# A two-layer Perceiver on one core: layer 0's start and order of work, and the last context chunk's values

## The chip, the cores and the metric

The kernel runs on one core of a Trainium2 chip. A core has five engines that work side by side and meet only through semaphores: TensorE (PE in the profile, its weight loads PEld), VectorE (DVE), ScalarE (ACT), GpSimd (POOL) and SyncE (SP), which here only issues DMAs. The metric is the device time of one execution in microseconds; before the change it is 2798.18 us, the median of 3 runs (2798.04 to 2798.63). All data are float32.

## The reference

The input is `x` (256 rows of 512) and a context of 25088 rows of 512. Two layers follow, each of three residual steps on a layer-normalized `x`. Cut to what matters:

```python
# layer 0
x = x + norm(x) @ W1.T + context.mean(0) @ W2.T + b              # "cross attention": a mean
x = x + banded_self_attention(norm(x))                            # 16 heads, window 128
x = x + moe(norm(x))                                              # 16 experts, top 4 of 2 groups of 4, and a shared one
# layer 1
q, K, V = norm(x) @ Wq + bq, context @ Wk + bk, context @ Wv + bv # 25088 keys, 16 heads of 32
x = x + softmax_over_queries(q K^T / sqrt(32)) V @ Wo + bo        # the softmax runs over the 256 queries
x = x + shifted_window_attention(norm(x))
x = x + moe2(norm(x))                                             # 8 experts, top 2
```

Because the softmax of layer 1's cross attention runs over the queries, each block of keys can be finished by itself: its probabilities are exact as soon as its scores are there, and all blocks are added.

## The kernel before, in words

**Context chunks.** The context is cut into 49 chunks of 512 rows. A chunk's keys and its values are each a 512 x 512 by 512 x 512 product, done as a 2 x 2 block product with seven half-size products instead of eight (`seven`, L528). One such product (`times`, L532) is 4 matmuls of 256 columns; an fp32 matmul leaves two records in the profile. The sums and differences of the context's blocks (`ts`) are made on GpSimd (`chunk_sums`, L517), those of the weight's blocks once on VectorE (`load_weights`, L492), in a tile `wq7` with seven blocks side by side; VectorE adds each product into its one or two targets (L559), GpSimd adds one bias difference (L563).

**Stage A, until about 186 us.** Layer 0 needs the mean over the whole context. Every chunk is loaded once for its column sums (`load_sum`, `chunk_sum`, ScalarE, L579) into buffers `ct` (three, used to the end of the context work) or `cs` (two); between them the keys and values of chunks 0 to 6 (`FIRST = 7`) are made from buffers `ck` (two) and stored to DRAM. Loads are issued by SyncE, stores by GpSimd.

**Stage B, layer 0.** The mean and `norm(x)` are multiplied with `l0x_w` (8 and 8 matmuls of 512 columns, L684). The self attention (`self_attention`, L218) and the expert layer follow. Chunks 7 and 8 (`NPRE = 9` in all) are made meanwhile, by a generator `early_rest`; `early_fill(n)` takes 2n products from it, at places where TensorE would have to wait for VectorE or ScalarE. The router picks the experts in order of their load: `slots` (L792) counts rows by expert with `low` and `ones`, ranks the counts and writes `expert_i`, by which SyncE addresses the loads of the experts' weights. `slots` is called inside the shared expert's `hidden` (L731), after its first third.

**Stage C, layer 1's cross attention.** 49 x 4 blocks of 128 keys, each in two halves of eight heads: 392 half-blocks. Each has 8 score matmuls (L1021), 8 exponentials on ScalarE (L1035) and 8 matmuls with the values (L1048). Between them run the products of chunks 9 to 48 (`projections`): a planner counts them in groups of 1, 2, 1, 2, 1 products and draws the lowest slopes under which each chunk's keys and values are made by the half-block that needs them (`due`, `plan`); values are due two half-blocks into their chunk. Chunk 48 is last, so its values are due at half-block 386.

**What sets the order.** Instructions written with `queue <<` keep their program order on their engine. All others (most VectorE work outside Stage C, all loads) are placed on their engine by a scheduler when their inputs and buffers are ready in its own simulation, lower in the program meaning lower priority; on the chip each engine then runs its list in that order. So a load may be issued before loads that are written ahead of it. Memory pools are opened and closed in scopes; a pool that takes memory of a closed one waits for that one's users. TensorE's list is written out nearly whole with `queue <<`.

Of the kernel before, what the change touches and what calls it, by code (L numbers as in the profile page):

```python
# [15 lines left out]
P = 128  # L16
# [21 lines left out]
def perceiver_kernel(  # L38
# [59 lines left out]
    def load_rows(pool, first, last):  # L98
# [15 lines left out]
    ident = const.tile([P, P], F32, name="ident")  # L114
    make_identity(nc, ident)
    eps = const.tile([P, 1], F32, name="eps")
    nc.vector.memset(eps, LN_EPS)

    tri = const.tile([P, NE0, NE0], F32, name="tri")
    nc.gpsimd.memset(tri, 1.0)  # L120
    nc.gpsimd.affine_select(
        out=tri, in_=tri, compare_op=ALU.is_ge, fill=0.0, base=-1,
        pattern=[[1, NE0], [-1, NE0]], channel_multiplier=0,
    )

    low, ones = (const.tile([P, P], F32, name=n) for n in ("low", "ones"))
    nc.gpsimd.memset(ones, 1.0)
    nc.gpsimd.affine_select(
        out=low, in_=ones, compare_op=ALU.is_ge, fill=0.0, base=-1,
        pattern=[[1, P]], channel_multiplier=-1,  # L130
    )
    iota = const.tile([P, P], F32, name="iota")

    band = const.tile([P, 2 * P], F32, name="band")
    nc.gpsimd.memset(band, 0.0)
    nc.gpsimd.affine_select(
        out=band, in_=band, compare_op=ALU.is_ge, fill=-1e30, base=-1,
        pattern=[[1, 2 * P]], channel_multiplier=-1,
    )
    nc.gpsimd.affine_select(  # L140
        out=band, in_=band, compare_op=ALU.is_ge, fill=-1e30, base=P,
        pattern=[[-1, 2 * P]], channel_multiplier=1,
    )
# [331 lines left out]
    ps = ps_mm([P, P])  # L475
    queue << nc.tensor.matmul(ps, ones, low, start=True, stop=True)
    nc.vector.tensor_copy(iota, ps)

# [10 lines left out]
    wq7 = kvp.tile([P, 2, 7, 2, HB], F32, name="wq7", bufs=1)  # L489
    W_A11, W_A12, W_A22, W_S1, W_S2, W_S3, W_S4 = range(7)  # L490

    def load_weights(k, matrix, ct=None, c=None):  # L492

        a21 = early.tile([P, 2, HB], F32, tag="a21", name="a21")
        for to, i, j in ((wq7[:, k, W_A11], 0, 0), (a21, 1, 0), (wq7[:, k, W_A22], 1, 1), (wq7[:, k, W_A12], 0, 1)):
            nc.sync.dma_start(out=to, in_=l1x_w_d[:, matrix, 2 * j : 2 * j + 2, HB * i : HB * (i + 1)])
            if ct is not None:
                nc.sync.dma_start(out=quarter(ct, j, i), in_=quarter(ctx_d[c], j, i))
        w = wq7[:, k]
        nc.vector.tensor_add(w[:, W_S1], a21, w[:, W_A22])  # L500
        nc.vector.tensor_sub(w[:, W_S2], w[:, W_S1], w[:, W_A11])
        nc.vector.tensor_sub(w[:, W_S3], w[:, W_A11], a21)
        nc.vector.tensor_sub(w[:, W_S4], w[:, W_A12], w[:, W_S2])
# [24 lines left out]
    def seven(ct, ts, out, is_key):  # L528

        w = wq7[:, 0 if is_key else 1]  # L530

        def times(a, b):  # L532
            ps, home = take("kv", [P, 2, HB])
            fixed, moving = (w[:, a], b) if is_key else (b, w[:, a])
# [55 lines left out]
    def early_load(c):  # L590
        if c < FIRST:
            ct = early.tile([P, DC, JC], F32, tag="ck", name="ck")
        else:
            ct = ctp.tile([P, DC, JC], F32, tag="ct", name="ct")
# [41 lines left out]
    early_load(1)  # L636
    rest = list(range(FIRST, NCH))
    for c in range(FIRST):
        units = early_chunk(c)
        n = min(8, len(rest)) if c + 1 < FIRST else len(rest)  # L640
# [7 lines left out]
        if c + 2 < FIRST:  # L648
            early_load(c + 2)
    early_scope.close()  # L650

    def early_rest():
        early_load(FIRST)
        for c in range(FIRST, NPRE):
            if c + 1 < NPRE:
                early_load(c + 1)
            yield from early_chunk(c)
# [7 lines left out]
    l0a_scope = ExitStack()  # L665
    l0w = l0a_scope.enter_context(tc.tile_pool(name="l0w", bufs=1))
    l0a_wo = l0w.tile([P, DC, D], F32, name="l0a_wo")
    with tc.tile_pool(name="l0xw", bufs=1) as l0xw:
        l0x_w = l0xw.tile([P, 2 * DC, D], F32, name="l0x_w")
        nc.sync.dma_start(out=l0x_w, in_=l0x_w_d)  # L670
        nc.sync.dma_start(out=l0a_wo, in_=l0a_wo_d)

        cmean = const.tile([P, DC], F32, name="cmean")
        nc.vector.tensor_reduce(cmean, csum, AX.X, ALU.add)
        nc.vector.tensor_scalar(cmean, cmean, 1.0 / (NCH * JC), None, ALU.mult)
        cmean_b = l0xw.tile([P, DC, P], F32, name="cmean_b")
        nc.vector.tensor_copy(cmean_b, cmean.unsqueeze(2).to_broadcast([P, DC, P]))

        xT = norm_T()
        pss = [ps_mm() for _ in range(T)]  # L680
        for k in range(2 * DC):
            for t in range(T):
                lhsT = xT[:, k, t * P : (t + 1) * P] if k < DC else cmean_b[:, k - DC, :]
                queue << nc.tensor.matmul(pss[t], lhsT, l0x_w[:, k, :], start=k == 0, stop=k == 2 * DC - 1)  # L684
        for t in range(T):
            add_rows(t, pss[t], R_L0X_B)
# [18 lines left out]

    NDENSE = (4 * NT) // (P + 1)
# [23 lines left out]
    def hidden(weights, between=lambda: None):  # L730
        w1, w3, w2 = weights  # L731
        hT = moe0.tile([P, IC0, NT], F32, tag="hT0", name="hT0")
        for ic in range(IC0):
# [10 lines left out]
            if ic == 0:  # L744
                between()
# [40 lines left out]
    early_fill(NPRE * 7)  # L786
# [662 lines left out]
```

## Time and profile before

| | |
|---|---|
| median of 3 runs | 2798.18 us (2798.04 to 2798.63) |
| the profiled execution: its time, its span | 2799.3 us, 2797.6 us |
| mean granted TensorE clock over the span | 0.987 |
| TensorE busy | 2721.9 us (97%) |
| VectorE, ScalarE, GpSimd busy | 1721.7, 1700.9, 577.5 us |
| DMA, mean | 94 GB/s; 422 GB/s from 20 to 160 us |
| Stage A, Stage B, Stage C | to 186 us, to 570 us, to 2455 us |

A line of waits tells which engine waited, at which line and for which tile, after the arrow who ended the wait, and the total, the number and the longest of the waits. A line of the timeline gives the start, the length, the engine, the line, the operation, output<-input and how many; in brackets the engine's idle time before it and what ended it. A line of stretches gives from:to, the length, the busy time and records of each engine, the granted TensorE clock, the DMA share and GB/s. Busy time of TensorE is modelled for pipelined matmuls, so the spacing of starts is the better measure of what a matmul costs.

### The profile page before, as it was taken

What the parts mean: (1) busy time and instruction counts of PE and PEld (TensorE: products, weight loads), DVE (VectorE), ACT (ScalarE), POOL (GpSimd) and SP (SyncE); (2) the same over time, 40 slices, a digit from 0 to 9 for tenths busy, and PEclk for the clock granted to TensorE, in tenths of its full rate; (3) what the DMA queues carried; (4) which work ended last, traced back from release to release, by engine and by line L of the source; (5) the groups of instructions that cost most, each with busy time, mean ns of one, the idle gap of its engine ahead of it and who ended that gap; (6) DMA issues with size and microseconds to landing.
All of it is one profiled execution on the core that took longest, in us unless ns stands there. A gap on an engine that the chain in (4) does not pass through costs nothing. (4 is left out here: it accounts for less than half of the span.)

```text
span 2797.6 us, 57238 instructions
## 1 busy us (share of the span) xinstructions
PE 2721.9 (97%) x21502; PEld 1920.9 (69%) x21502; DVE 1721.7 (62%) x3052; ACT 1700.9 (61%) x7001; POOL 577.5 (21%) x529
## 2 busy tenths in 40 slices
PE   8998899999999999999999999999999999979997
PEld 7866777776666666666666666666666666656775
DVE  4436512267777777777777777777777777742101
ACT  6832100037877777777777778777887778831111
POOL 4321000023222223222222232222222323100000
PEclk9999999999999999999999999999999999989999
DMA  9961344421100101000101000101000100107673
GB/s 387 423 266 76 134 160 170 162 91 41 37 32 32 41 22 47 32 32 32 46 17 47 32 32 32 46 17 47 32 32 32 47 17 27 51 24 297 259 271 145
DMA packets 40869, 262.87 MB, mean 94 GB/s; under 512 B 5320, under 2 KB 8440, under 8 KB 13200
## 3 DMA queue, kind: packets, MB, share of 16 engines
q1 hardware_dynamic: 37408, 237.85, 22.6%
q0 software_dynamic: 3184, 21.33, 1.9%
q8 instruction: 175, 2.87, 0.4%
q14 instruction: 102, 0.84, 0.1%
HBM read 239.23 MB, written 19.40 MB: 92 GB/s over the span
## 5 line engine op out<-in xcount | busy, mean ns | idle before, releaser
L1035 ACT ACTIVATE e<-ps_sc,nm 128x256 f32<-128x256 f32 x3136 | 1437.8, 485 | 377.4 <-DVE nm L1030 376.9
L1030 DVE TENSOR_REDUCE nm<-ps_sc 128x2 f32<-128x512 f32 x1568 | 995.3, 686 | 358.0 <-PE ps_sc L1021 357.9
L1035 ACT ACTIVATION_READ_ACCUMULATOR e<-ps_sc,nm 128x1 f32 x3136 | 678.7, 216 | 0.0
L1048 PE MATMUL ps_ac<-e,vs 128*32 128x256 f32 x6272 | 420.7, 386 | 4.1 <-POOL vs L1062 4.1
L537 PE MATMUL ps_kv<-ts,wq 128*128 128x256 f32 x1568 | 387.1, 391 | 5.8 <-POOL ts L523 5.8
L537 PE MATMUL ps_kv<-wq,ts 128*128 128x256 f32 x1568 | 388.8, 392 | 0.0
L1062 POOL TENSOR_TENSOR vs<-v,rc 128x512 f32<-128x512 f32 x160 | 167.8, 1049 | 1016.3 <-DVE rc L1056 1016.3
L537 PEld LDWEIGHTS ps_kv<-ts,wq 128*128 128x128 f32 x1568 | 286.1, 190 | 91.1 <-issue 27.3
L537 PEld LDWEIGHTS ps_kv<-wq,ts 128*128 128x128 f32 x1568 | 287.2, 191 | 85.2 <-issue 26.5
L1021 PE MATMUL ps_sc<-qT,kT 32*128 32x256 f32 x4096 | 304.1, 401 | 1.5 <-ACT e L1035 1.3
L1048 PEld LDWEIGHTS ps_ac<-e,vs 128*32 128x32 f32 x6272 | 164.2, 109 | 202.2 <-issue 114.1
L559 DVE TENSOR_TENSOR v<-v,ps_kv 128x512 f32<-128x512 f32 x343 | 227.7, 677 | 82.6 <-PE ps_kv L537 58.1
L1021 PEld LDWEIGHTS ps_sc<-qT,kT 32*128 32x128 f32 x4096 | 191.4, 184 | 116.5 <-ACT e L1035 106.4
L537 PE MATMUL ps_kv<-wq,ct 128*128 128x256 f32 x1008 | 244.2, 385 | 0.0
L537 PE MATMUL ps_kv<-ct,wq 128*128 128x256 f32 x1008 | 242.4, 383 | 0.0
L559 DVE TENSOR_TENSOR kT<-kT,ps_kv 128x512 f32<-128x512 f32 x280 | 187.1, 681 | 68.4 <-PE ps_kv L537 58.4
L537 PEld LDWEIGHTS ps_kv<-wq,ct 128*128 128x128 f32 x1008 | 189.7, 191 | 38.2 <-ACT e L1035 12.9
L537 PEld LDWEIGHTS ps_kv<-ct,wq 128*128 128x128 f32 x1008 | 188.1, 190 | 38.1 <-ACT e L1035 12.6
L1338 ACT ACTIVATE hT<-ps_mm,b 128x128 f32<-128x128 f32 x128 | 36.6, 368 | 210.5 <-PE ps_mm L1332 157.3
L1021 PE MATMUL ps_sc<-qT,kTp 32*128 32x256 f32 x2176 | 156.9, 400 | 0.0
L523 POOL TENSOR_TENSOR ts<-ct 128x512 f32<-128x512 f32 x84 | 107.1, 1275 | 230.9 <-DMA ct<-in_ctx_dram 230.9
L1021 PEld LDWEIGHTS ps_sc<-qT,kTp 32*128 32x128 f32 x2176 | 99.6, 184 | 58.7 <-ACT e L1035 55.2
(273 smaller groups left out, 2180.2 us busy)
## 6 DMA issues: line engine op xcount, KB each, us to landing
ct<-in_ctx_dram SPq DMA_DIRECT2D x67, 1024.0 KB, 5.0
we<-in_l1e_dram SPq DMA_DIRECT2D x64, 1024.0 KB, 6.8
we<-in_l0e_dram SPq DMA_DIRECT2D x17, 1536.0 KB, 8.1
cs<-in_ctx_dram SPq DMA_DIRECT2D x17, 1024.0 KB, 14.6
we0o<-in_l0e_dram SPq DMA_DIRECT2D x17, 768.0 KB, 4.5
kv<-kT POOLq DMA_DIRECT2D x9, 1024.0 KB, 9.7
kv<-v POOLq DMA_DIRECT2D x9, 1024.0 KB, 9.4
vp<-kv SPq DMA_DIRECT2D x9, 1024.0 KB, 4.8
```

Source lines behind the costliest of these rows:

```text
L523: queue << nc.gpsimd.tensor_sub(ts[:, k], a, b)
L537: queue << nc.tensor.matmul(ps[:, m, :], fixed[:, d, m * P : (m + 1) * P], moving[:, d, :], start=d == 0, stop=d == 1,)
L559: queue << nc.vector.tensor_tensor(to, old, ps, ALU.subtract if a == W_A22 else ALU.add)
L1021: queue << nc.tensor.matmul(sc[r][:, i, :], kTs[c][part, 2 * qp + i, s * P : (s + 1) * P], qT[part, 2 * qp + i, :], start=True, stop=True,)
L1030: queue << nc.vector.tensor_reduce(nm[:, 2 * qp : 2 * qp + 2, r], sc[r], AX.X, ALU.max, negate=True)
L1035: queue << nc.scalar.activation(e[:, 4 * i + r, :], sc[r][:, i, :], AF.Exp, bias=nm[:, q, r : r + 1], accum_out=sm[:, q, r : r + 1],)
L1048: queue << nc.tensor.matmul(acc[qp][32 * r : 32 * r + 32, i, :], v[:, h * HD : (h + 1) * HD], es[qp][:, 4 * i + r, :], start=first and i = ...
L1062: queue << nc.gpsimd.tensor_mul(vs.rearrange("p (h d) -> p h d", h=H), vs_of[c, s].rearrange("p (h d) -> p h d", h=H), rc.unsqueeze(2).to_ ...
L1338: nc.scalar.activation(hT[:, fc, :], ps[:, fc, :], AF.Gelu, bias=b1[:, hf * FC + fc : hf * FC + fc + 1])
```

## The change

It does the following.

- `load_weights` loads each weight, and chunk 0 with it, in two halves of 256 input rows in place of four quarters. The quarters are now read in place, out of a tile `whole`; only the four sums are kept apart (`sums`). The seven blocks side by side and the tiles `a21` go.
- The constants for GpSimd (`ident`, `tri`, `low`, `ones`, `band`) are made by `make_constants`, called after the first loads have been written. The small product that makes `iota` moves from the kernel's start to behind the self attention.
- Chunk 6 leaves the loop of Stage A: its buffer is a `ct`, and its 14 products are now the first of `early_rest`.
- The pools of `l0a_wo` and `l0x_w` are opened before that loop. After it `norm_T` transposes `norm(x)`, nine products of chunk 6 run, then the product of `norm(x)` with `l0x_w`, row block by row block. The mean is multiplied once (4 matmuls) and added to both row blocks, in place of a product for each. Its broadcast lies in a `tmp` buffer.
- In the expert layer four products run, then `slots`, then all products left, then the shared expert. `picked` shares `gt`'s buffer. The copy of `to` goes from VectorE to ScalarE.
- The values of chunk 48 are made block by block: 8 products of 4 matmuls (128 keys, 256 columns) in place of seven, in groups of one, the two of each block due by the block's end.

```diff
-    ident = const.tile([P, P], F32, name="ident")
-    make_identity(nc, ident)
...
+    def make_constants():
+        make_identity(nc, ident)
+
+        nc.gpsimd.memset(tri, 1.0)
...
-    ps = ps_mm([P, P])
-    queue << nc.tensor.matmul(ps, ones, low, start=True, stop=True)
-    nc.vector.tensor_copy(iota, ps)
...
-    wq7 = kvp.tile([P, 2, 7, 2, HB], F32, name="wq7", bufs=1)
+    whole = [kvp.tile([P, DC, D], F32, name=f"whole{k}", bufs=1) for k in range(2)]
+    sums = [kvp.tile([P, 4, 2, HB], F32, name=f"sums{k}", bufs=1) for k in range(2)]
...
+    def weight(k, a):
+        if a >= W_S1:
+            return sums[k][:, a - W_S1]
+        return quarter(whole[k], int(a == W_A12 or a == W_A22), int(a == W_A22))
...
-        a21 = early.tile([P, 2, HB], F32, tag="a21", name="a21")
-        for to, i, j in ((wq7[:, k, W_A11], 0, 0), (a21, 1, 0), (wq7[:, k, W_A22], 1, 1), (wq7[:, k, W_A12], 0, 1)):
-            nc.sync.dma_start(out=to, in_=l1x_w_d[:, matrix, 2 * j : 2 * j + 2, HB * i : HB * (i + 1)])
+        for j in range(2):
+            half = slice(2 * j, 2 * j + 2)
+            nc.sync.dma_start(out=whole[k][:, half, :], in_=l1x_w_d[:, matrix, half, :])
             if ct is not None:
-                nc.sync.dma_start(out=quarter(ct, j, i), in_=quarter(ctx_d[c], j, i))
...
+                nc.sync.dma_start(out=ct[:, half, :], in_=ctx_d[c][:, half, :])
+        a21 = quarter(whole[k], 0, 1)
...
     def early_load(c):
-        if c < FIRST:
+        if c + 1 < FIRST:
             ct = early.tile([P, DC, JC], F32, tag="ck", name="ck")
...
     early_load(1)
+    make_constants()
+    l0a_scope = ExitStack()
+    l0w = l0a_scope.enter_context(tc.tile_pool(name="l0w", bufs=1))
+    l0a_wo = l0w.tile([P, DC, D], F32, name="l0a_wo")
+    l0xw_scope = ExitStack()
+    l0xw = l0xw_scope.enter_context(tc.tile_pool(name="l0xw", bufs=1))
+    l0x_w = l0xw.tile([P, 2 * DC, D], F32, name="l0x_w")
     rest = list(range(FIRST, NCH))
-    for c in range(FIRST):
+    for c in range(FIRST - 1):
...
+    nc.sync.dma_start(out=l0x_w, in_=l0x_w_d)
+    early_load(FIRST)
+
+    xT = norm_T()
+
     def early_rest():
-        early_load(FIRST)
+        yield from early_chunk(FIRST - 1)
...
-        pss = [ps_mm() for _ in range(T)]
-        for k in range(2 * DC):
-            for t in range(T):
-                lhsT = xT[:, k, t * P : (t + 1) * P] if k < DC else cmean_b[:, k - DC, :]
-                queue << nc.tensor.matmul(pss[t], lhsT, l0x_w[:, k, :], start=k == 0, stop=k == 2 * DC - 1)
-        for t in range(T):
-            add_rows(t, pss[t], R_L0X_B)
+    for _ in range(9):
+        next(unmade)
+
+
+    for t in range(T):
+        ps = ps_mm()
+        for k in range(DC):
+            queue << nc.tensor.matmul(
+                ps, xT[:, k, t * P : (t + 1) * P], l0x_w[:, k, :], start=k == 0, stop=k == DC - 1
+            )
+        add_rows(t, ps, R_L0X_B)
+
+    nc.sync.dma_start(out=l0a_wo, in_=l0a_wo_d)
...
+    cmean_b = work.tile([P, D], F32, tag="tmp", name="cmean_b").rearrange("p (c j) -> p c j", c=DC)
+    nc.vector.tensor_copy(cmean_b, cmean.unsqueeze(2).to_broadcast([P, DC, P]))
+    ps = ps_mm()
+    for k in range(DC):
+        queue << nc.tensor.matmul(ps, cmean_b[:, k, :], l0x_w[:, DC + k, :], start=k == 0, stop=k == DC - 1)
+    for t in range(T):
+        nc.vector.tensor_add(x[:, t, :], x[:, t, :], ps)
+    l0xw_scope.close()
...
+    ps = ps_mm([P, P])
+    queue << nc.tensor.matmul(ps, ones, low, start=True, stop=True)
+    nc.vector.tensor_copy(iota, ps)
...
-    early_fill(NPRE * 7)
-    store()
+    early_fill(2)
...
-        picked = mini([P, T, NE0, NE0], "picked")
+        picked = moe0.tile([P, T, NE0, NE0], F32, tag=f"gt{NE0}", name="picked", bufs=1)
...
-    pending = [*hidden(shared_weights, between=slots), None]
+    slots()
+    early_fill(NPRE * 7)
+    store()
+    pending = [*hidden(shared_weights), None]
...
-        nc.vector.tensor_copy(to, tp)
+        nc.scalar.copy(to, tp)
...
+        def values_by_block(c, ct, v):
+
+            for s in range(SUB):
+                for j in range(2):
+                    half = slice(HB * j, HB * (j + 1))
+                    ps, home = take("kv", [P, HB])
+                    for d in range(DC):
+                        queue << nc.tensor.matmul(
+                            ps, ct[:, d, s * P : (s + 1) * P], whole[1][:, d, half],
+                            start=d == 0, stop=d == DC - 1,
+                        )
+                    queue << nc.vector.tensor_add(v[:, s, half], ps, rows[R_L1X_BV][:, half])
+                    give(home)
+                    if j == 1:
+                        made.add(("v", c, s))
+                    yield
...
+                if k + 1 == len(late):
+                    yield from values_by_block(c, cts[k], v)
+                    break
...
-        groups, done = (1, 2, 1, 2, 1), 0
-        total = 2 * len(groups) * len(late)
+        groups, done = (1, 2, 1, 2, 1) * (2 * len(late) - 1) + (1,) * (2 * SUB), 0
+        total = len(groups)
...
-                due += [(2 * SUB * at, k + len(groups)), (2 * SUB * at + 2, k + 2 * len(groups))]
+                k = 10 * (c - NPRE)
+                due.append((2 * SUB * at, k + 5))
+                if c == late[-1]:
+                    due += [(2 * SUB * at + 2 * s, k + 5 + 2 * s) for s in range(1, SUB + 1)]
+                else:
+                    due.append((2 * SUB * at + 2, k + 10))
```

## Prediction

> **What bounds the kernel now.** I read the page first, for the engine that is full:
>
> ```profile
> span 2797.6 us, 57238 instructions
> PE 2721.9 (97%) x21502; PEld 1920.9 (69%) x21502; DVE 1721.7 (62%) x3052; ACT 1700.9 (61%) x7001; POOL 577.5 (21%) x529
> ...
> PE   8998899999999999999999999999999999979997
> ```
>
> TensorE is busy nearly all the time, so time is won only by removing TensorE work or one of its few gaps; a faster VectorE or GpSimd buys nothing by itself. The low digits lie in slices 1, 4 to 6 and 37, that is at the start, around 180 to 350 us and after the context attention. Next, TensorE's waits, whose columns are line, tile, releaser, then total, times and longest:
>
> ```profile
> PE ps_mm L737 <- DMA we<-in_l0e_dram: 6.3, 1, 6.3
> PE ps_mm L476 <- POOL low L128: 6.1, 1, 6.1
> PE ps_kv L537 <- POOL ts L523: 5.8, 2, 5.4
> PE ps_mm L684 <- issue: 5.3, 1, 5.3
> PE ps_ac L1048 <- POOL vs L1062: 4.1, 1, 4.1
> PE ps_mm L198 <- DMA l0a_wqkv<-in_l0a_wqkv_dram: 3.4, 1, 3.4
> ```
>
> All six touch edited code. The 5.3 at L684 is put down to issue, but the load of `l0x_w` was issued at 185.06 and lands 7.5 us later, at 192.6; the matmul starts at 192.81. It is that load. The third view is busy time by stretch (PE, PEld, DVE, ACT, POOL, clock, DMA share, GB/s):
>
> ```profile
> 150.00:160.00 10.00, 10.00 (x48) 8.81 (x47) 2.50 (x4) 8.33 (x28) 0.00 (x0) 1.00 1.01 423
> 186.00:193.00 7.00, 1.72 (x13) 1.38 (x12) 1.91 (x4) 0.00 (x0) 0.00 (x0) 0.89 0.82 300
> 193.00:199.50 6.50, 6.50 (x10) 2.68 (x11) 0.00 (x0) 0.00 (x0) 0.00 (x0) 0.59 0.00 0
> 199.50:209.30 9.80, 9.80 (x24) 4.34 (x23) 0.62 (x1) 0.00 (x0) 0.00 (x0) 1.00 0.01 2
> 338.00:350.00 12.00, 5.72 (x18) 4.71 (x18) 1.73 (x8) 0.38 (x1) 0.00 (x0) 0.72 0.98 390
> ```
>
> In the context stage DMA is as full as TensorE (1.01). After a gap the granted clock is 0.59: 10 matmuls in 6.5 us, then 24 in 9.8. A gap is paid twice.
>
> **Units.** An fp32 matmul leaves two records. One product of `seven` (8 records, 256 columns) takes 1.73 us (0.216 each); a 512-column record takes 0.43.
>
> **Part 1, start and context stream: 3.7 us.** The first product starts at 6.71, the second at 15.72, waiting for `ts` and then at half clock; from 21.56 on products follow each other every 1.73. Afterwards nothing waits for `low`, and the first four loads are halves. The quarters flowed at 302, 210, 165, 242, 277, 301, 323, 361 GB/s in the eight us from 2 to 10, where whole chunks give 422; DMA share 0.99 gave 323. With 6 issues (0.5 us each) in place of 12 and longer rows I take 400, so 1 MB more has come by 10 us: the stream is 2.4 us ahead. Both halves of both operands land near 9. GpSimd now issues the 0.56 us row load before its constants, which end near 8.0 in place of 7.36; two subtractions of 1.28 put `ts1` at 10.6, the second product near 11, and the fourth near 15 to 16, some 5.5 us sooner.
> The SBUF page of the Trainium skill (SBUF — State Buffer, section The DMA setup-cost knee) speaks against larger pieces where the first bytes count: fixed 2 us plus bytes at 436 GB/s. By it the first pair of quarters is there at 0.82 + 2 + 1.2 = 4.0, a pair of halves at 5.2, a loss of 1.2 us. The row puts the first product at 6.71, and the second, which needs nearly all pieces, at 15.72, so I go by the row.
> TensorE can't keep the 5.5, since the stream bounds chunk 6:
>
> ```profile
> 143.34 0.68 SPq L598 DMA_DIRECT2D ck<-in_ctx_dram  x1
> ...
> 160.15 1.27 POOL L523 TENSOR_TENSOR ts<-ck 128x512 f32<-128x512 f32 x1 [16.71 <-PE ps_kv L537]
> ...
> 163.94 1.99 PE L537 MATMUL ps_kv<-ts,wq 128*128 128x256 f32 x8 [0.42 <-POOL ts L523]
> ```
>
> It lands at 160 for use at 161.4. In a `ct` buffer it takes the place issued at 146.06 but has the same loads ahead; with the stream 2.4 ahead, it lands near 157.5. Two subtractions later (160.2) its second product starts, not at 163.94: 3.7. Below: -2 if chunk 6 lands 5 us late; above: 6.
>
> **Part 2, the mean's turn: 12.5 us.** The 8 transposes (1.04 us) now run before chunk 6, where TensorE would wait anyway: 1.0. Then nine products bring TensorE to 174. `l0x_w` no longer waits for the early buffers (SyncE waited 19.4 us there); behind the last sum it lands at 168 to 174, as `l0a_wo`, issued at 151.35, landed at 167.5. Gone: the gap, 5.3, and the slow clock, 16.5 us for 32 records at 0.43 = 13.7, so 2.8. The TensorE page of the Trainium skill (TensorE: Matmul & The Clock Gate, section HAM oscillation) charges about 1.7 us of half rate per such wait, which would give 0.9 lost in place of 2.8; the row decides. Mean product: 4 matmuls in place of 8, 8 x 0.43 = 3.4. The column sums, their broadcast and two added VectorE sums (0.69 each, one replaced bias addition less) lie beside the x products. If `l0x_w` is late, everything behind it in TensorE's fixed order is, by the same time: range 4 to 8.1 for that term.
>
> **Part 3, qkv weights: 1.4 us.** Issued at 209.53 after L684's last read, used at 220.68; `xT` was ready at 218.5, so 2.2 are to be had. The narrower `l0xw` pool may let it go ahead of the mean product; I can't see the placement: 0 to 2.2, two chances in three, 1.4. The attention keeps 18 products in the same places, one phase of `seven` earlier: no change, plus or minus 3 (its 3.1 us wait for VectorE at 274 may move).
>
> **Part 4, routing: 8.2 us.** The experts' load leaves at 336.95, 1 us after `expert_i`, and lands at 344.3; TensorE waits 6.3 from 338 and then takes 12.64 us for 48 records worth 10.35: 2.3 more. Now four products cover the choice (`sel` at 322.1, products until 323.1), the counting follows, and seven products (12.1) plus the whole shared hidden layer (10.4) come after it. VectorE's chain took 5.0 us, so `expert_i` is there by 330 and the weights by 338.5; TensorE wants them at 347. 8.6, less 0.4 for a possible wait for `sel`. Ends: 2 (VectorE puts the products' additions first) and 8.6. `picked` in `gt`'s buffer stays on one engine: nothing. The copy of `to` on ScalarE: 0.42 on VectorE, 0.37 for L289's like form: nothing. `iota`'s product moves, 0.25 us, no sum.
>
> **Part 5, the last chunk: 7.0 us.**
>
> ```profile
> 2405.59 1.07 PE L1048 MATMUL ps_ac<-e,vs 128*32 128x256 f32 x16
> ...
> 2411.32 1.07 PE L1048 MATMUL ps_ac<-e,vs 128*32 128x256 f32 x16
> ...
> 2415.32 1.07 PE L1048 MATMUL ps_ac<-e,vs 128*32 128x256 f32 x16
> ...
> 2434.73 1.07 PE L1048 MATMUL ps_ac<-e,vs 128*32 128x256 f32 x16
> ...
> 2438.38 1.07 PE L1048 MATMUL ps_ac<-e,vs 128*32 128x256 f32 x16
> ...
> 2451.68 3.31 PE L1048 MATMUL ps_ac<-e,vs 128*32 128x256 f32 x32 [4.05 <-POOL vs L1062]
> ```
>
> A half-block with two products takes 5.73, with one 4.00, without any 3.65 (2434.73 to 2438.38), which is ScalarE's eight exponentials, though TensorE's own work is 2.08. Values due by half-block 386 leave six without products. The plan is the same up to half-block 346; then 40 half-blocks held 40 groups, 16 of them double (40 x 4.00 + 16 x 1.73 = 187.7, as the trace has it), and six ran at ScalarE's pace (24 us from 2426.09 to the last exponential, 2449.96). Afterwards 46 hold 43 groups, 14 double, three empty: 43 x 4.00 + 14 x 1.73 + 3 x 2.08 + 1.5 for ScalarE's debt = 204, and 1.6 to the last exponential. 187.7 + 23.9 - 205.6 = 6.0, the eighth product (1.73) included. TensorE's last wait shrinks below 3 us, so the final 32 records need 2.3 in place of 3.3: 1.0. The third `wct` load now waits for the last chunk's buffer until near 2442; 5.5 us later it is there, used past 2480: hidden.
>
> **Sum.** 3.7 + 12.5 + 1.4 + 8.2 + 7.0 = 32.8. The profiled run took 2799.3 (span 2797.6), 1.1 over the median of the runs shown. 2798.2 - 32.8 = 2765.4; I say 2766.
>
> **Rivals.** (a) *The stream takes it back.* `l0x_w` and `l0a_wo` (3.1 MB) need no early buffer now and may be issued ahead of chunk 6: 3.1 MB at 422 GB/s is 7.4 us, and a long gap brings 2.8 of slow clock: 2766 + 10 = 2776. For it: share 1.01. Against: `l0a_wo` was issued behind the last sum. 20%. (b) *The routing wait stays*, because additions delay the slot chain on VectorE, or waits in layer 0's attention grow: 2766 + 8 = 2774; 10%. (c) *Slower.* The weight quarters are now read with a row stride of 512 in place of packed. Three of seven products use them, 49 chunks x 2 x 3 = 294. If each cost over 0.11 us more (6%), the 32.8 is gone; at 0.15 it ends at 2766 + 44 = 2810. Against: `ct` quarters are strided so today, and L537's forms with `ct` and with `ts` take 385 and 391 ns. With anything else of that sign 7%. (d) *No change:* 2%. (e) *More*, chunk 6 earlier and attention smoother: 2756, 3%. The main case has 58%, own range 2757 to 2775.
>
> **From this** the range is 2754 to 2784, with (a) and (b) inside and nearly all of (c) outside. A measurement of this kernel tells about 0.2%: faster 0.90, same 0.03, slower 0.07.
>
> **What would show it.** Right: no 6 us wait at L737's later place, none over 1 us for `l0x_w`; second product near 11; chunk 6's second product near 160; half-blocks of 4.0 to the end of L1048. Wrong: DMA waits of L537 on `ts` or `ct` between 130 and 165, L537 records over 0.22 us, or a wait for `sel` at L458 over 2 us.

## The result, and the profile after

The changed kernel takes 2775.73 us, the median of 4 runs from 2773.82 to 2777.49, against 2798.4 us before on the same chip: a ratio of 0.9919, interval 0.9907 to 0.9931. Run again later, it took 2775.08. The forecast was 2766, range 2754 to 2784: the sign and the range held, but of the 32.8 us it added up, 22.7 came.

The page of the profiled execution (which took 2775.05 us):

```profile
span 2773.4 us, 57230 instructions
...
PE 2710.4 (98%) x21502; PEld 1919.4 (69%) x21502; DVE 1715.3 (62%) x3045; ACT 1702.8 (61%) x7010; POOL 574.6 (21%) x528
...
PE   8998999999999999999999999999999999979997
```

TensorE has as many records as before and is busy for 11.5 us less. 1.7 of it is 8 records of 512 columns in the mean product that became 8 of 256 in the last chunk's eighth product; the rest is slow clock that went. Its waits (line, tile, releaser; total, times, longest):

```profile
...
PE ps_kv L541 <- DMA ck<-in_ctx_dram: 6.7, 1, 6.7
PE ps_ac L1089 <- POOL vs L1103: 5.6, 4, 3.8
...
PE ps_kv L541 <- POOL ts L528: 3.2, 1, 3.2
...
PE ps_mm L702 <- DVE cmean_b L699: 1.2, 1, 1.2
```

The waits of 6.3 for the first expert's weights, of 5.3 for `l0x_w` and of 3.4 for `l0a_wqkv` are gone. The long wait ahead of the last attends is still there (3.8), and one is new: the mean product for `cmean_b`.

Where the time was won is read from places that both traces have. Until the routing TensorE has made five products less than before (8.63 us of work, made later); they are taken off.

| place | before | after | lead, products taken off | forecast |
|---|---|---|---|---|
| chunk 6's second product | 163.94 | 162.29 | 1.7 | 3.7 (+1.0 of transposes) |
| end of the mean product | 209.34 | 187.85 | 12.9 | 16.2 |
| first qkv matmul | 220.68 | 196.94 | 15.1 | 17.6 |
| router's logits | 312.48 | 288.01 | 15.8 | 17.6 |
| outputs of the first expert | 356.82 | 331.70 | 25.1 | 25.8 |
| first context scores | 596.31 | 571.08 | 25.2 | 25.8 |
| last attends | 2451.68 | 2424.06 | 27.6 | 31.8 |
| end of the span | 2797.6 | 2773.4 | 24.2 | 32.8 |

Up to the context attention the sum is right to 0.6 us, partly by luck: the stretches miss by -2.0, -1.3, +0.8, +0.7 and +1.1 and cancel. The miss is the last two lines: Part 5 brought 2.4 in place of 6.0, and behind it 3.4 us of lead were lost where 1.0 was to be won. Of the 10.1 us missing, that is 3.6 and 4.4; 0.6 lie ahead, and 1.5 between these two executions and the medians.

The timeline of the changed kernel (start, length, engine, line, operation, tiles, records, idle before and its releaser) at the start and at chunk 6:

```profile
11.93 1.34 POOL L528 TENSOR_TENSOR ts<-ck,ts 128x512 f32<-128x512 f32 x1 [3.30 <-DMA ck<-in_ctx_dram]
...
13.32 3.53 PE L541 MATMUL ps_kv<-ts,sums 128*128 128x256 f32 x8 [3.19 <-POOL ts L528]
...
157.18 1.26 POOL L528 TENSOR_TENSOR ts<-ct 128x512 f32<-128x512 f32 x1 [17.11 <-DMA ct<-in_ctx_dram]
...
158.41 1.27 POOL L567 TENSOR_TENSOR v<-v,dbv 128x512 f32<-128x512 f32 x1
...
160.46 2.00 PE L541 MATMUL ps_kv<-ct,whole 128*128 128x256 f32 x8 [1.15 <-DVE v L563]
```

The second half of the first chunk lands at 11.9, not near 9. Chunk 6 lands at 157.1, as forecast (157.5); but GpSimd, in its fixed order, stood 17 us at chunk 6's difference with chunk 5's bias addition queued behind it. So chunk 5's values were finished late, their bank of PSUM (the memory that TensorE writes to) came free late, and chunk 6 waited 1.15 for it.

The same view at one of the half-blocks without a product, and at the end of the context attention:

```profile
2283.03 1.15 PE L1062 MATMUL ps_sc<-qT,kT 32*128 32x256 f32 x16
2284.85 1.07 PE L1089 MATMUL ps_ac<-e,vs 128*32 128x256 f32 x16 [0.68 <-POOL vs L1103]
2285.85 0.89 PE L1062 MATMUL ps_sc<-qT,kT 32*128 32x256 f32 x6
2286.96 1.13 PE L1062 MATMUL ps_sc<-qT,kT 32*128 32x256 f32 x10 [0.22 <-ACT e L1076]
2288.02 2.00 PE L541 MATMUL ps_kv<-whole,ct 128*128 128x256 f32 x8
2289.94 1.07 PE L1089 MATMUL ps_ac<-e,vs 128*32 128x256 f32 x16
2290.94 1.15 PE L1062 MATMUL ps_sc<-qT,kT 32*128 32x256 f32 x16
...
2424.06 3.64 PE L1089 MATMUL ps_ac<-e,vs 128*32 128x256 f32 x32 [3.83 <-POOL vs L1103]
2427.63 8.14 PE L214 MATMUL ps_mm<-wts,oT 128*128 128x512 f32 x16
...
2441.47 9.77 PE L332 MATMUL ps_mm<-xT,wct 128*128 128x256 f32 x32 [0.78 <-DVE xT L184]
```

From 2283.03 to 2290.94 lie two half-blocks, one without a product and one with a single one: 7.91 us, so the first is not had for TensorE's own 2.08; the two cost as much as two with a product (4.00 each) less 0.09. Meanwhile, from 2284.98 to 2288.59, ScalarE starts an exponential every 0.45 us. At the end, the 32 records of the last attends take 3.64 us, where the 32 before them took 1.93. The windows (span; busy PE, PEld, DVE, ACT, POOL; granted clock, DMA share, GB/s) of the changed kernel:

```profile
2424.00:2428.00 4.00, 3.94 (x33) 1.75 (x34) 0.90 (x2) 0.00 (x0) 0.01 (x1) 0.50 0.00 0
2428.00:2436.00 8.00, 7.99 (x18) 3.42 (x17) 2.94 (x6) 0.29 (x1) 0.00 (x0) 0.89 0.00 0
```

and of the kernel before, at the same work:

```profile
2451.70:2455.00 3.30, 3.30 (x33) 1.46 (x33) 0.69 (x1) 0.00 (x0) 0.00 (x0) 0.57 0.00 0
2455.00:2462.00 7.00, 7.00 (x18) 3.17 (x18) 2.95 (x5) 0.30 (x1) 0.00 (x0) 1.00 0.00 0
```

About 3 us at half clock before, over 5 us after, behind waits of 4.05 and 3.83 us.

### The profile page after: what moved, and what is told of

Its sections match the earlier page's. It is cut to its first block, busy times and chain, and to the rows that moved or that the text cites. A ratio compares the mean times of both kernels' runs of the same rounds, so it can differ in the third digit from the quotient of the medians.

```text
span 2773.4 us, 57230 instructions
## 1 busy us (share of the span) xinstructions
PE 2710.4 (98%) x21502; PEld 1919.4 (69%) x21502; DVE 1715.3 (62%) x3045; ACT 1702.8 (61%) x7010; POOL 574.6 (21%) x528
## 5 line engine op out<-in xcount | busy, mean ns | idle before, releaser
L1062 PE MATMUL ps_sc<-qT,kT 32*128 32x256 f32 x4096 | 298.2, 401 | 0.4 <-ACT e L1076 0.2
L541 PE MATMUL ps_kv<-ts,sums 128*128 128x256 f32 x1176 | 291.5, 393 | 3.3 <-POOL ts L528 3.2
L541 PE MATMUL ps_kv<-sums,ts 128*128 128x256 f32 x1152 | 282.7, 390 | 0.0
L541 PEld LDWEIGHTS ps_kv<-ts,sums 128*128 128x128 f32 x1176 | 216.4, 192 | 66.4 <-ACT e L1076 23.5
L541 PEld LDWEIGHTS ps_kv<-sums,ts 128*128 128x128 f32 x1152 | 210.3, 190 | 61.0 <-ACT e L1076 23.9
L541 PE MATMUL ps_kv<-ct,whole 128*128 128x256 f32 x688 | 166.8, 385 | 1.1 <-DVE v L563 1.1
L541 PE MATMUL ps_kv<-whole,ct 128*128 128x256 f32 x672 | 164.9, 389 | 0.0
L541 PEld LDWEIGHTS ps_kv<-ct,whole 128*128 128x128 f32 x688 | 127.7, 190 | 30.2 <-ACT e L1076 12.6
L541 PEld LDWEIGHTS ps_kv<-whole,ct 128*128 128x128 f32 x672 | 125.7, 192 | 29.2 <-ACT e L1076 12.6
```

Source lines behind the costliest of these rows:

```text
L541: queue << nc.tensor.matmul(ps[:, m, :], fixed[:, d, m * P : (m + 1) * P], moving[:, d, :], start=d == 0, stop=d == 1,)
L1062: queue << nc.tensor.matmul(sc[r][:, i, :], kTs[c][part, 2 * qp + i, s * P : (s + 1) * P], qT[part, 2 * qp + i, :], start=True, stop=True,)
```

## The experiments

My theory after the two traces: Parts 1 to 4 gave what the table says; Part 5 failed on two terms, the price of a half-block without a product and the clock behind the last wait. The rivals: that the values by block cost something themselves, or that the tail is one run's chance.

**The changed kernel again.**

> The changed kernel itself, for the comparison with the runs beside it: 2775.7, last attends near 2424, 3.4 us more from there to the end than the kernel before. If its slow clock behind the last wait was one run's chance, those 3.4 us are under 1 here; if it is the position of that wait, 32 records take 3.6 again.

2775.08 us (2774.6 to 2775.4). The 32 records took 3.64 again. That does not tie the slow clock to the place: with Part 4 undone (below), the same 32 records behind the same wait (3.84) took 2.52. And from the last attends at 2422.70 to the end of the span, 2773.7, it took 351.0 us, where the first execution took 349.3 and the kernel before 345.9: the same instructions of one kernel differ by 1.7 us in the tail.

**Part 5 undone.**

```
-                if k + 1 == len(late):
-                    yield from values_by_block(c, cts[k], v)
-                    break
-        groups, done = (1, 2, 1, 2, 1) * (2 * len(late) - 1) + (1,) * (2 * SUB), 0
+        groups, done = (1, 2, 1, 2, 1) * (2 * len(late)), 0
```

> The changed kernel with one part undone: the values of the last context chunk again by seven products in groups (1,2,1,2,1), all due before its first half-block. The forecast's theory: the part is worth 7.0 us, so this takes 2775.7 + 7.0 = 2782.7, and its last 32 attend records take 3.3 us. Theory from the two traces: the part is worth 2.4 at the last attends, which start here near 2426.5 in place of 2424.06, and nothing after them; 2776 to 2779. Rival: the slow clock that the changed kernel shows behind the last wait (32 records in 3.64 us where the kernel before took 3.31, 1.0 us more in the output projection, 1.4 more in the first hidden layer of layer 1) comes from the new shape of the end; then it is gone here and this takes 2773 to 2775, no longer than the changed kernel.

2774.43 us (2772.61 to 2774.84): as the rival said, no longer than with Part 5. Its reason came only in part: the output projection is back at 7.13, the 32 records are not. Its last attends:

```profile
2426.95 3.46 PE L1088 MATMUL ps_ac<-e,vs 128*32 128x256 f32 x32 [4.06 <-POOL vs L1102]
2430.34 7.13 PE L214 MATMUL ps_mm<-wts,oT 128*128 128x512 f32 x16
```

From the first scores (571.41) to them it took 1855.5 us, against 1853.0 with Part 5: the part is worth 2.6 there. From them to the end 345.9, as in the kernel before, against 349.3. In these two traces the part wins 2.6 and the tail behind it loses 3.4.

The other traces confirm the first number and not the second. From the first scores to the last attends the four traces without the part take 1854.5 to 1855.6 us, the six with it and with its half-blocks as they were 1853.0 to 1853.1. But the tail, where no wait is covered, took 345.9 to 348.3 us without the part and 348.3 to 351.0 with it (347.9 with the half-blocks filled); Part 1 alone and Part 4 undone, one of each sort, both took 348.3. So it is not shown that Part 5 costs the tail anything.

**No half-block without a product.**

```
+        phases = [(1, 2, 1, 2, 1)] * (2 * len(late) - 1) + [(1,) * (2 * SUB)]
+        for p in (73, 76, 78):
+            phases[p] = (1, 2, 1, 1, 1, 1)
```

> The changed kernel with three double groups among the last seven phases split in two, so that each of the last 86 half-blocks has at least one product (in the changed kernel the 362nd, the 378th and the last have none). The forecast's theory prices an empty half-block at TensorE's own 2.08 us, so filling one saves a double (1.73) and costs 4.00 - 2.08 = 1.92: no gain, 0.6 us slower, 2776.3. Theory from the trace: an empty half-block with its neighbour took 7.91 us, so it costs 3.9, ScalarE's pace: two of them filled save 2 x (1.73 - 0.09) = 3.3, the last one 1.73 at most where its product falls into the wait ahead of the last attends: last attends near 2419 to 2421 in place of 2424.06, and 2771 to 2773.

2769.77 us (2766.4 to 2770.8), 5.3 under the changed kernel's 2775.08. By the forecast's price it should have gained nothing. At the same place and at the end:

```profile
2281.94 1.19 PE L1066 MATMUL ps_sc<-qT,kT 32*128 32x256 f32 x16
...
2285.98 1.15 PE L1066 MATMUL ps_sc<-qT,kT 32*128 32x256 f32 x16
...
2289.98 1.15 PE L1066 MATMUL ps_sc<-qT,kT 32*128 32x256 f32 x16
...
2420.71 1.93 PE L1093 MATMUL ps_ac<-e,vs 128*32 128x256 f32 x32 [2.39 <-POOL vs L1107]
2422.62 7.13 PE L214 MATMUL ps_mm<-wts,oT 128*128 128x512 f32 x16
```

Two half-blocks with a product each take 8.04 us, with one product more in them than the 7.91 held. From the first scores (571.21) the last attends come after 1849.5 us, 3.5 sooner than in the changed kernel: 3.3 for two filled half-blocks was expected. The third one's product runs inside the last wait and makes it 2.39 us, and behind it the 32 records take 1.93: 1.7 more (by luck of where that wait falls, as the last section shows).

**The last wait covered.**

```
+        ps, home = take("kv", [P, HB])
+        for k in range(8):
+            queue << nc.tensor.matmul(ps, whole[1][:, 0, :P], whole[1][:, 1, :HB], start=k == 0, stop=k == 7)
+        give(home)
         for qp in range(2):
             attend(*pending[0], qp, *pending[1])
```

> The changed kernel with 8 matmuls of 256 columns that nothing reads (16 records, 3.5 us at full clock) put into TensorE's 3.83 us wait ahead of the last attends. Theory: idling there is what slows the clock, so with it covered the last 32 records take 1.95 us in place of 3.64, the 16 records of the output projection 7.0 in place of 8.1, and part of what follows is saved: 2772 to 2773. Rival: the wait is short and the clock behind it is set by something else, or the 2.5 us gaps behind it slow it in any case: 2775 to 2776. If the extra matmuls run past the wait they cost what they overrun, under 1 us.

2770.44 us (2769.18 to 2771.31).

```profile
2421.45 3.72 PE L1169 MATMUL ps_kv<-whole 128*128 128x256 f32 x16
2425.36 1.93 PE L1089 MATMUL ps_ac<-e,vs 128*32 128x256 f32 x32 [0.19 <-POOL vs L1103]
2427.27 7.13 PE L214 MATMUL ps_mm<-wts,oT 128*128 128x512 f32 x16
```

With work in the wait the records run at full clock, 1.71 and 1.01 us less. That is 2.7 of the 5.1 that its tail is shorter (344.2 from the last attends); the rest fell off at later slow places, the 32 records at L332 (9.04 for 9.77) and the first hidden layer's (3.81 for 5.32), which this cover doesn't touch.

To separate the two, the same cover was put on the kernel without Part 5.

> The changed kernel with the last chunk's values by seven products again, and its wait ahead of the last attends covered by 16 records, as in the run that covered it with the values by block (2770.4). Theory: the part is worth the 2.6 us at the last attends, and what made it worth nothing was the slow clock behind a wait; with the wait covered in both, this takes 2.6 longer, 2773.0. Rival: the part is worth nothing in any case: 2770.4. Both show 32 records in 1.9 us.

2775.23 us (2774.58 to 2775.58): longer than either said. The last attends come 1855.6 us after the first scores, against 1853.0 in the run above, so Part 5's 2.6 stands. The 32 records take 1.93, yet the tail is 346.6 us, no better than uncovered (345.9): here the first hidden layer's records fell into the slow clock (5.31). So a cover at one wait alone is worth its own 1.5 to 2.7 us; what comes behind, plus or minus 2, depends on how the next waits fall.

**All waits behind the context attention covered.** A helper issues matmuls that nothing reads, by the length of each wait:

```
+    def cover(n):
+        ps = ps_mm([P, 2 * P])
+        for k in range(n):
+            queue << nc.tensor.matmul(ps, ident, band, start=k == 0, stop=k == n - 1)
...
+    xT = norm_T(roll=64, covers=(5, 1))
+    cover(1)
...
+    xT = norm_T(untransposed=xns, covers=(4, 4))
...
+    cover(4)
     places, counts = places_of(ep, keep, NE1)
...
+            cover(7)
         xg = gathered(which[0])
+            cover(2)
```

> The changed kernel with matmuls that nothing reads in the waits behind the context attention: 16 records ahead of the last attends as in the run with that wait covered, and 2 to 14 records, by the length of each wait, ahead of the four transposes of the window attention and of the router, ahead of the first hidden projection of the window attention, ahead of the counting of the choice, ahead of the first gathering and ahead of the first expert's hidden layer. Theory: the slow clock behind these waits is what 9.77 us for 32 records (6.9 at full clock), 3.42 for the router's 16, 3.78 for 16 records of the gathering (1.95 later) show; covered, some 2 to 2.8 us at the window attention and 3 to 4 at the routing go besides the 5 of the last wait: 2763 to 2766. Rival: those operations are slow for their own reasons, and only the last wait counts: 2770.4, or more where the extra matmuls overrun.

2768.11 us (2766.37 to 2768.72). The tail is 341.2 us, 8.1 under the changed kernel's.

```profile
2439.89 7.17 PE L339 MATMUL ps_mm<-xT,wct 128*128 128x256 f32 x32 [0.35 <-DVE xT L191]
...
2480.99 2.01 PE L478 MATMUL ps_mm<-l1g_w,xT 128*128 128x8 f32 x16
...
2489.86 2.02 PE L1311 MATMUL ps_mm<-g,xn 128*128 128x128 f32 x16 [0.34 <-DVE g L1305]
2491.72 1.03 PE L171 MATMUL ps_mm<-band,ident 128*128 128x256 f32 x4
2494.69 5.44 PE L1395 MATMUL ps_mm<-xg,we 128*128 128x128 f32 x32 [1.94 <-DVE at L1301]
```

The covered places run as fast as the records allow: 7.17 for 9.77, 2.01 for 3.42, 2.02 for 3.78. The last cover was too short, and there the slow clock came (5.44). Of the 2 to 5 us that the gain falls short of the expectation, 1.6 are this and 1.3 lie ahead of the first scores (572.36 for 571.08).

**Part 4 undone** (the choice counted inside the shared hidden layer again).

```
-    slots()
-    early_fill(NPRE * 7)
-    store()
-    pending = [*hidden(shared_weights), None]
+    pending = [*hidden(shared_weights, between=slots), None]
```

> The changed kernel with one part undone: the choice of experts is counted again inside the shared expert's hidden layer, behind its first block, and all remaining products of the context run ahead of that layer. The forecast's theory: 6.3 us of wait and 2.3 of slow clock come back and 0.4 for the choice goes, so it takes 8.2 longer than the changed kernel, 2783.9. Theory from the two traces, which put the part at 9.4 (25.1 us of lead behind the first outputs, 15.1 at the attention's weights, 1.0 won in between, 0.4 for other things): 2785, with a wait of 6 us for the weights of the first expert. Rival: part of the gain came from elsewhere (weights that land sooner because the start is 25 us earlier), then the wait is shorter than 5 us and the time under 2782.

2781.7 us (2778.16 to 2783.52), 6.6 more than 2775.08.

```profile
327.37 12.00 PE L759 MATMUL ps_mm<-xT,we 128*128 128x256 f32 x48 [5.80 <-DMA we<-in_l0e_dram]
```

The wait is back with 5.80 (the rival wanted it under 5) and its slow clock with 12.00 - 10.35 = 1.65: 7.45. From the router's logits to the first expert's outputs it takes 51.84 us against 43.69, 8.15 more. Some of that is chance: right behind the logits this execution has 16 records in 5.38 us, the changed kernel's in 3.70. The run with the filled half-blocks has the slow 16 too (5.39) and takes 44.41 there; against that, Part 4 is worth 7.4. The forecast said 8.2. The 9.3 of my table holds 1.15 from the longer wait in the kernel before.

**Part 1 alone**, in the kernel before (loads in halves, whole weights, constants behind the second chunk's load; with them the new places of `iota`'s product and of `picked`).

> The kernel before with the first part of the change alone: loads of the first weights and the first chunk in halves, weights kept whole with strided quarters, constants behind the second chunk's load. The forecast's theory: second product near 11, chunk 6's second product near 160 in place of 163.94, 3.7 us: 2794.5. Theory from the trace of the changed kernel: the second halves land only at 11.9, the second product starts near 13.3, chunk 5 ends 3.4 sooner, and chunk 6 keeps 1.7 to 3.4 of it: 2794.5 to 2796.5, with chunk 6 in its old place and buffer. Rival: the stream of context loads is full and takes it all back: 2797.7. Second rival: the strided quarters cost more than they bring, and the time is over 2798.

2797.3 us, ratio to before 0.9998 (0.9989 to 1.0007), from 2792.95 to 2800.5 over 11 runs. By the interval it is worth between -2 and +3.1 us in that kernel; the forecast's 3.7 lies outside. In its profiled execution the second product starts at 13.47 and chunk 6's second product at 161.14, 2.8 sooner than before, with the wait for `l0x_w` behind it 5.68 in place of 5.3. The strided quarters don't show as a cost. Why this kernel's runs spread over 7.5 us is open.

**Two orders mended.**

```
-                if part == 1 and c + 1 in loaded:
+                if part == 1 and n > 0 and c + 1 in loaded:
-    cmean_b = work.tile([P, D], F32, tag="tmp", name="cmean_b").rearrange("p (c j) -> p c j", c=DC)
+    cmean_b = work.tile([P, D], F32, tag="xn", name="cmean_b").rearrange("p (c j) -> p c j", c=DC)
```

> The changed kernel with two orders mended. First, a chunk's first GpSimd difference for the next chunk is put behind the bias addition of the chunk in hand, so that it no longer stands in that queue waiting for the load of chunk 6. Theory: then the VectorE evictions of chunk 5 come on time, the 1.15 us wait of chunk 6's first product goes, and its second product starts near 161.1 in place of 162.29. Rival: the load itself sets chunk 6 (it landed at 157.1), and nothing is gained there. Second, the mean's columns take the buffer of a normalised tile in place of one of the two buffers of the bias additions, so VectorE makes them before those. Theory: the 1.2 us wait of the mean product goes. Both: 2773.3. If each only moves the wait to the next matmul: 2775.7.

2773.53 us (2772.57 to 2776.29), inside the noise of 2775.08, but the trace shows both:

```profile
158.98 1.04 PE L181 MATMUL ps_mm<-ident,xn 128*128 128x128 f32 x8
159.85 1.89 PE L541 MATMUL ps_kv<-ct,whole 128*128 128x256 f32 x8
161.58 1.89 PE L541 MATMUL ps_kv<-ts,sums 128*128 128x256 f32 x8
```

Chunk 6's wait is gone although this execution came to it 0.7 later, and the mean product starts at 182.26 for 184.34 with no wait and ends at 185.69 for 187.85, 2.2 sooner. The first scores, at 568.67, are 2.4 sooner than in the changed kernel's first execution, but only 0.95 sooner than in its second (569.62).

**All together.** The orders, the filled half-blocks and the covers (10 records ahead of the last attends).

> All mended at once: the two orders, the half-blocks without a product filled, the waits behind the context attention covered (10 records ahead of the last attends, since that wait is only 2.4 us then). If the gains add: 2.4 of the orders, 4.8 of the half-blocks with their faster last records, 5 to 7 of the later covers: 2760 to 2763. If the covers only repeat what the filled half-blocks won: 2766 to 2768.

2765.59 us (2763.05 to 2766.73); the wait ahead of the first hidden layer was 2.19 behind its 4 records of cover, and its 32 records took 5.44. With `cover(6)` there:

> All mended as before, with the cover ahead of the first expert's hidden layer of 12 records in place of 4, since 1.0 us of cover there left a wait of 2.2 and 5.44 us for 32 records. Theory: 12 records fill 2.6 of 3.2 us, and the 32 records take 3.8: 1.6 us less than the 2765.6 measured, 2764.0. If the weights' landing sets that place, the wait stays as long in sum and only the slow clock goes.

2760.69 us (2760.41 to 2761.91), ratio to before 0.9867 (0.9852 to 0.9882), 14.4 under the changed kernel measured beside it and the best of all.

```profile
2487.01 3.81 PE L1399 MATMUL ps_mm<-xg,we 128*128 128x128 f32 x32 [0.29 <-DVE at L1305]
```

The 1.6 expected are there; the other 3 us between the medians lie earlier (the profiled executions differ by 2.2 at the first scores, with the same instructions).

**The start's clock covered too.**

```
+    cover_early(8)
     early_load(0)
+            if c == k == 0:
+                cover_early(9)
```

> The same, and the slow clock of the start covered: 16 records ahead of the first product and 18 between the first and the second, from a tile that VectorE sets. The first product then takes 1.9 in place of 3.7, the second 1.9 in place of 3.6, and the fourth starts near 15.4 in place of 18.4 to 19.5. Forecast's theory (the context stream bounds chunk 6): chunk 6's second product, at 161.6 with the orders mended, gains 1 to 2 at most and the time 1 to 2: 2762 to 2763. Rival (TensorE bounds the stretch from 20 to 160, since the loads have slack): all 3 to 4 us stay, 2760 to 2761. Third: the extra matmuls delay the first product or the loads are late anyway: 2764 or more.

2763.73 us (2762.92 to 2764.91), slower by 3.0. The first products run at full clock (1.96 and 1.99), but the second half of the first chunk lands at 13.0 in this execution, where 12.0 beside it, and the lead is 0.75 us from there to the qkv weights, 1.85 at the first scores (566.35) and at the last attends. So the covered start itself gave under 1 us with the loads late, as in the third case; the further 1.1 came between the qkv weights and the first scores, where two executions of one kernel differ as much. Behind the attends:

```profile
2459.69 0.35 PE L407 MATMUL ps_mm<-pT_wa,v_swapped 64*32 64x64 f32 x7 [1.97 <-DMA v_swapped<-v_wa]
...
2461.02 9.59 PE L221 MATMUL ps_mm<-wts,oT_wa 128*128 128x512 f32 x16
```

The last small transfer of `v_swapped` comes 4.1 us after its issue, where 2.4 beside it, and the projection behind it runs slow (9.59 for 7.11): 4.3 us lost. Why that transfer was late was not found, nor whether it was late in the other three executions.

## Why the prediction was right or wrong

The range held, the middle did not: 2775.73 is 9.7 over 2766, about where rivals (a) and (b) would have put it (2776 and 2774), and neither of them came. The range was wide because of them; that the result lies inside is in good part luck.

**Parts 2, 3 and 4 were right.** Part 2: 12.9 - 1.7 = 11.2 where 12.5 were forecast. The gap for `l0x_w`, its slow clock and half the mean product went as worked out, `l0x_w` was issued at 153.09 behind the last sum, and rival (a), the stream taking it back, didn't come. The missing 1.2 is the wait for `cmean_b`, which the forecast put "beside the x products": it overlooked that the tile shares its two buffers with the bias additions and so comes behind one of them on VectorE; another buffer removes it. Part 3: 2.2, the upper of its two ends, where I took 1.4. Part 4: 7.4 to 8.15 against 8.2. The attention, "no change, plus or minus 3", gave 0.7 in this pair.

**Part 1 was half wrong.** The step that failed is "both halves of both operands land near 9". The early rate was counted for the first chunk alone, but what is issued behind it takes its share: by the GB/s of the first 12 us 3.4 MB had moved when the second half (issued at 2.21) was there, and the chunk and its weights are 2.1 of them. The rate was too high as well: 323 GB/s on average from 2 to 10 us, where 400 was taken. So the second product gained 2.4 in place of 4.7. (The first starts at 6.74 for 6.71: the 1.2 us that larger pieces might have cost there did not come.) The bound that the forecast then used, chunk 6's landing, was right (157.1 for 157.5); the step from there, "two subtractions later", left out what was queued on GpSimd between them. 1.7 in place of 3.7; mended, it gives 2.2 by the end of the mean product, together with `cmean_b`.

**Part 5 was wrong**, and with what lies behind it holds 8.0 of the 10.1 us missed. Two terms of the sum failed. The first is "three empty: 3 x 2.08". A half-block without a product costs 3.9, because eight exponentials of ScalarE (its 3.65, which the forecast itself had read from the row) follow each other through it; filling two of them won 3.5 us. With 3.9 for two of the three the forecast's 205.6 becomes 209.2 and Part 5's 6.0 becomes 2.4, which is what came. The second is "TensorE's last wait shrinks below 3 us, so the final 32 records need 2.3". TensorE runs out of work at 2420.23 while ScalarE is still at the last half-block's exponentials; the last of their sums is there at 2422.44, and the reciprocal and GpSimd's scaling follow, until 2424.06. Nothing in Part 5 gave TensorE work in that time, and the wait stayed at 3.83. A filled last half-block did shorten it, to 2.39. And the 32 records took 3.64 in place of the 2.3 forecast.

**What lay behind was not in the sum.** A wait before the end doesn't cost the same each time: from the last attends to the end the same work took 345.9 to 351.0 us in the eight traces without a cover, 344.2 and 346.6 in the two with one, and 341.0 to 345.3 in the four with all. The forecast took the tail as constant. That is 3.4 of its miss; the kernel before, with 345.9, happened to have the shortest of the eight.

Of the rivals, (b) and (c) didn't come: no routing wait above 0.73, and with the same other operand the forms with the strided `whole` take 385 and 390 ns, those with the packed `sums` 380 and 393. Of the signs named as "wrong" none appeared, but two of those named as "right" did not appear either: the second product came at 13.32, not near 11, and chunk 6's at 162.29, not near 160. The sign "half-blocks of 4.0 to the end" appeared, and was no proof of the 6.0. One reading was off without consequence: the low digits of TensorE's row lie in slices 1, 4, 5, 36 and 40.

## What to carry to other kernels

When work is moved into a paced stretch, price the slots that it leaves empty by the slowest engine of the slot, not by the engine that you are relieving, and spread the work so that no slot is empty. Treat each longer wait of TensorE (here 2 to 4 us) as two costs, the wait and the slow records behind it, and where the wait can't go, fill it with matmuls that nothing reads, up to a few tenths of its end; do so for all waits in a row, since one cover leaves the others to chance. On an engine with a fixed order, ask what stands behind each instruction that waits for a load.

## What the runs showed of the hardware that I had not expected

Behind a wait of 3.83 us the granted clock was 0.50 for 4 us and 0.89 over the next 8; behind 2.39 us it stayed at 1.00. Behind a cover of 1.0 us and a wait of 1.94 it fell to 0.68 over 5.3 us, so the length of the last wait alone doesn't decide.

What does can be read off the traces. In all 14 the clock is granted at 1.00 or 0.50, and every slow stretch that ends within the span is 3.41 us or a whole multiple of it long; within a trace all their edges lie on one grid of 3.41 us, which stands differently to the program's start from trace to trace. Cut on that grid, the time around the last attends (columns as above) is, in the changed kernel, with Part 4 undone, and with the half-blocks filled:

```profile
2419.44:2422.86 3.42, 0.79 (x16) 0.22 (x8) 1.20 (x3) 3.40 (x15) 0.00 (x0) 1.00 0.36 135
2422.86:2426.27 3.41, 2.21 (x24) 1.06 (x28) 0.18 (x1) 0.88 (x1) 1.05 (x1) 0.50 0.00 0
2426.27:2429.68 3.41, 3.41 (x19) 1.34 (x12) 1.20 (x2) 0.00 (x0) 0.00 (x0) 0.50 0.00 0
...
2425.99:2429.40 3.41, 1.79 (x32) 0.79 (x26) 1.94 (x4) 3.17 (x15) 0.00 (x0) 1.00 0.66 255
2429.40:2432.82 3.42, 1.21 (x24) 0.78 (x28) 0.29 (x2) 1.87 (x5) 1.05 (x1) 1.00 0.00 0
2432.82:2436.23 3.41, 3.41 (x19) 1.38 (x12) 1.34 (x2) 0.00 (x0) 0.00 (x0) 0.50 0.00 0
2436.23:2439.64 3.41, 3.41 (x9) 1.49 (x9) 0.74 (x2) 0.00 (x0) 0.00 (x0) 1.00 0.00 0
...
2416.22:2419.63 3.41, 2.10 (x34) 0.94 (x32) 1.49 (x4) 3.39 (x15) 0.02 (x1) 1.00 0.42 126
2419.63:2423.04 3.41, 2.33 (x33) 1.23 (x34) 0.99 (x2) 0.76 (x1) 1.02 (x1) 1.00 0.47 182
```

A wait of 3.83 us that falls as in the first leaves TensorE busy for only 0.79 us of one stretch, and two slow ones follow. The wait of 3.84 in the second is split 1.79 to 1.21, and one follows. The wait of 2.39 in the third leaves over 2 us of work in both stretches, and none follows. Over all traces, from 25 us on, each of the 61 full-clock stretches in which TensorE was busy for under 1.4 us was followed by a slow one; of some 11000 with more, 24 were, and why those were is open.

The same instructions in two executions of the changed kernel had a clock of 0.72 and of 1.00 between 228 and 234 us, with 16 records in 5.22 and 3.69 us. The Trainium skill (TensorE: Matmul & The Clock Gate, section HAM oscillation) charges about 1.7 us of throttled time per such wait, half of it lost; here the one wait of 3.83 us made the two groups behind it take 1.71 and 1.01 us more.
